# Graph attention in blocks of 1024 targets, with the two float16 halves summed in the same PSUM columns and the pair ends off GpSimd

## The chip, the cores and the metric

The kernel runs on one core of a Trainium2 chip. The metric is the device time of one execution in microseconds (us). A time given here is the median of an execution's repetitions, with the lowest and highest behind it. All runs compared here were in the fast state (mean granted TensorE clock 0.976 to 0.987 over the span, and 0.946 to 0.948 in e3).

## The reference, cut to what matters

Two graph attention (GAT) layers over 4096 nodes with 256 features and 8 heads of 32, then one transformer layer with the same adjacency. All is float32.

```python
def _gat_layer(x, adj_mat, W, a):
    Wh = jnp.einsum('nd,hdo->hno', x, W)
    src = jnp.einsum('hno,ho->hn', Wh, a[:, :O])
    dst = jnp.einsum('hno,ho->hn', Wh, a[:, O:])
    e = jax.nn.leaky_relu(src[:, :, None] + dst[:, None, :], LRELU_SLOPE)   # 0.2
    e = jnp.where(adj_mat[None, :, :] > 0, e, NEG_INF)
    alpha = jax.nn.softmax(e, axis=-1)
    out = jnp.einsum('hnm,hmo->hno', alpha, Wh)
    return jnp.transpose(out, (1, 0, 2)).reshape(N, -1)
h = jax.nn.elu(_gat_layer(x, adj_mat, W1, a1)) + x
out = jax.nn.elu(_gat_layer(h, adj_mat, W2, a2)) + h
# ... then layer norm, masked attention, projection, MLP
```

The kernel never forms the exponentials for all pairs of nodes. Where `src_n + dst_m >= 0` the weight is `exp(src_n) exp(dst_m)`, elsewhere `exp(0.2 src_n) exp(0.2 dst_m)`. So it needs only the 0/1 matrix "the sum is at least zero", masked by the adjacency, and multiplies it by rows that already carry `exp(dst)` or `exp(0.2 dst)`. Those rows are kept as two float16 halves, high and low, to come near float32.

## The kernel before

A block of targets is four or six tiles of 128. For each pair of heads (j = 0, 1) it runs over 32 tiles of sources (m), in groups of four. VectorE makes head 0's compares, ScalarE head 1's (as a sign), and VectorE ands them with the mask:

```python
TILES = (4, 6, 6, 6, 6, 4)
...
LO = 2048.0; V1 = O + 1; VW = 4 * V1        # 132: form 1 high, low, form 2 high, low
...
for i in range(G):                           # compare(), one group of four source tiles
    mt = g * G + i
    nc.vector.tensor_scalar(t8[:, i, 0, :n], s_b[:, 0, :n], L.negd[:, mt, 2 * p : 2 * p + 1],
                            None, op0=ALU.is_ge, saturate=False)
    nc.scalar.activation(t8[:, i, 1, :n].bitcast(I8), s_b[:, 1, :n], AF.Sign,
                         bias=L.negd[:, mt, 2 * p + 1 : 2 * p + 2], scale=-1.0)
    if i % 2 == 1:
        # ... both = two source tiles, both heads, as int32
        nc.vector.tensor_tensor(both, both, m32..., op=ALU.bitwise_and)
```

TensorE then does three matmuls for each target tile and source tile, 132 columns each, into one bank of PSUM (the memory in which matmuls accumulate) for each target tile:

```python
for n in range(TILES[nb]):
    for m in range(G):
        for j in range(2):
            nc.tensor.matmul(acc[n][:, j * VW : (j + 1) * VW], t8[:, m, j, at],
                             vst[g][:, m, 2 * p + j, :], start=(mt == 0 and j == 0), stop=False)
        nc.tensor.matmul(acc[n][:, 2 * VW : 3 * VW]..., masks[l, nb][mt // MC][:, mt % MC, at],
                         vst[g][:, m, 2 * p : 2 * p + 2, 2 * V1 :], start=False, stop=(mt == NT - 1))
```

ScalarE then copies the sums out of PSUM (the "evictions" below). The pair end adds the halves, combines, divides and applies the activation. It runs beside the next pair's work:

```python
nc.vector.scalar_tensor_tensor(halves[:, :, :V1], halves[:, :, V1:], 1.0 / LO, halves[:, :, :V1], ...)
nc.gpsimd.tensor_tensor(y, over, ev[...], op=ALU.subtract)
nc.gpsimd.tensor_tensor(y, y, L.r[...], op=ALU.mult)
nc.gpsimd.tensor_tensor(y, y, ev[...], op=ALU.add)
# ... check, reciprocal on VectorE
nc.gpsimd.tensor_tensor(z, y[:, :, :, :O], inv..., op=ALU.mult)
nc.vector.tensor_scalar(low, z, 0.0, None, op0=ALU.min)
nc.scalar.activation(th, low, AF.Tanh, scale=0.5)
nc.scalar.activation(low, low, AF.Exp)
nc.vector.scalar_tensor_tensor(th, low, 1.0, th, op0=ALU.add, op1=ALU.mult)
nc.vector.scalar_tensor_tensor(th, z, 0.0, th, op0=ALU.max, op1=ALU.add)
nc.gpsimd.tensor_tensor(th, th, x, op=ALU.add)
```

## Time and profile before

The time is 3616.01 us (3614.03 to 3619.31). The stages, from the times of the pairs' last evictions and of the first and last scores in the trace:

| stage | ends at, us |
|---|---|
| GAT layer 1 (first block's start and preparation included) | 986.9 |
| GAT layer 2, last matmul | 1862.6 |
| layer norms and projections, until the first scores | 2012.1 |
| last scores | 3315.9 |
| end | 3617.8 (the profiled execution) |

The change touches the first two rows directly. The groups of instructions that matter there are these, from the page's costliest groups. Engines are PE (TensorE's matmuls), PEld (its weight loads, one before each matmul), DVE (VectorE), ACT (ScalarE) and POOL (GpSimd); SPq is SyncE's queue of DMA transfers. The columns are line, engine, operation, output and input by name, shapes, count; then busy time and the mean nanoseconds of one; then the idle time before them and what ended most of it.

```profile
L1225 PE MATMUL bank<-vst,t 128*128 128x132 f16 x16384 | 1498.8, 221 | 108.0 <-DVE t L1031 78.9
L1021 ACT ACTIVATE t<-s_b,g_negd 128x768 int8<-128x768 f32 (+1 forms) x1536 | 1198.5, 854 | 73.3 <-PE bank L1225 61.7
L1013 DVE TENSOR_SCALAR t<-s_b,g_negd 128x768 fp8e4<-128x768 f32 (+1 forms) x1536 | 914.4, 647 | 7.2 <-PE bank L1225 6.2
L1031 DVE TENSOR_TENSOR t<-t,mask 128x768 int32<-128x768 int32 (+1 forms) x768 | 652.2, 869 | 1.9 <-DVE e_inv L1091 0.3
L1077 POOL TENSOR_TENSOR e_y<-ev 128x396 f32<-128x396 f32 (+1 forms) x48 | 95.0, 1980 | 1061.2 <-DVE ev L1067 1043.7
```

TensorE's matmuls waited 78.9 us for VectorE's ands, while VectorE's ands and compares waited 9 us in all: VectorE holds the layers up. The last line is one of GpSimd's five operations of a pair end.

### The profile page before, as it was taken

To read this page: it belongs to the slowest core of one execution; us is meant where nothing else is said; L and a number is where in the kernel's file an instruction comes from. 1 tells how busy PE (TensorE), PEld (TensorE's weight loads), DVE (VectorE), ACT (ScalarE), POOL (GpSimd) and SP (SyncE) were. 2 spreads that over 40 slices of the span, in tenths; PEclk is the share of its full clock that TensorE was granted. 3 is DMA by queue.
4 is the path that set the end of the run, shared out by engine and by line. 5 is a ranking of instruction groups with operands and counts; after the bars stand their busy time and mean duration, and the time that the engine had idled before them with its cause. 6 is when DMAs were issued, how large, how long until landed. Compare 5 with 4: busy or idle time off the path is not lost. (4 is left out here: it accounts for less than half of the span.)

```text
span 3617.8 us, 84393 instructions
## 1 busy us (share of the span) xinstructions
PE 3338.1 (92%) x35522; PEld 2088.3 (58%) x35522; DVE 3119.3 (86%) x4361; ACT 2694.2 (74%) x3603; POOL 1572.3 (43%) x778
## 2 busy tenths in 40 slices
PE   6899999999888999999978799999999999997999
PEld 4789998998768999999865111111111121111666
DVE  6999999999999999999972799999999999997211
ACT  5898888888768787878764677777777777775422
POOL 0112221122101112121210699999999999997110
PEclk9999999999999999999989899999999999999999
DMA  5463334433212121211126301101010101002110
GB/s 160 139 190 115 121 117 153 123 96 88 63 40 69 32 72 37 67 54 38 35 65 157 82 25 24 39 12 44 15 36 19 30 25 24 25 7 71 41 47 25
DMA packets 224375, 237.16 MB, mean 66 GB/s; under 512 B 103728, under 2 KB 183088, under 8 KB 223984
## 3 DMA queue, kind: packets, MB, share of 16 engines
q1 hardware_dynamic: 223984, 231.66, 22.5%
q8 instruction: 280, 4.59, 0.5%
q14 instruction: 111, 0.91, 0.1%
HBM read 189.15 MB, written 42.47 MB: 64 GB/s over the span
## 5 line engine op out<-in xcount | busy, mean ns | idle before, releaser
L1225 PE MATMUL bank<-vst,t 128*128 128x132 f16 x16384 | 1498.8, 221 | 108.0 <-DVE t L1031 78.9
L1232 PE MATMUL bank<-vst,mask 128*128 128x132 f16 x8192 | 1467.4, 221 | 0.0
L1225 PEld LDWEIGHTS <-t 128*128 128x128 fp8e4 x16384 | 1270.1, 96 | 148.7 <-DVE t L1031 106.4
L1578 POOL TENSOR_TENSOR u_both<-u_e 128x1024 f32<-128x1024 f32 x512 | 1200.0, 2367 | 251.6 <-DVE u_e L1487 251.4
L1487 DVE SCALAR_TENSOR_TENSOR u_e<-u_mask,u_ps 128x1024 f32<-128x1024 uint8 x1024 | 1202.0, 1216 | 98.1 <-ACT u_ps L1485 93.6
L1021 ACT ACTIVATE t<-s_b,g_negd 128x768 int8<-128x768 f32 (+1 forms) x1536 | 1198.5, 854 | 73.3 <-PE bank L1225 61.7
L1485 ACT ACTIVATE u_ps<-u_ps 128x1024 f32<-128x1024 f32 x1024 | 1010.9, 1008 | 293.5 <-PE u_ps L1478 274.6
L1013 DVE TENSOR_SCALAR t<-s_b,g_negd 128x768 fp8e4<-128x768 f32 (+1 forms) x1536 | 914.4, 647 | 7.2 <-PE bank L1225 6.2
L1232 PEld LDWEIGHTS <-mask 128*128 128x128 fp8e4 x8192 | 808.9, 99 | 0.6
L1031 DVE TENSOR_TENSOR t<-t,mask 128x768 int32<-128x768 int32 (+1 forms) x768 | 652.2, 869 | 1.9 <-DVE e_inv L1091 0.3
L1478 PE MATMUL u_ps<-u_q,u_k 128*128 128x512 f16 x2048 | 579.0, 384 | 36.8 <-DMA u_q<-half_d 21.0
L1478 PEld LDWEIGHTS <-u_k 128*128 128x128 f16 x2048 | 139.1, 97 | 742.4 <-issue 683.8
L1077 POOL TENSOR_TENSOR e_y<-ev 128x396 f32<-128x396 f32 (+1 forms) x48 | 95.0, 1980 | 1061.2 <-DVE ev L1067 1043.7
L1492 PE MATMUL u_av<-u_e,u_v 128*32 128x512 f32 x4096 | 546.3, 605 | 0.0
L1492 PE MATMUL u_dn<-u_both,u_ones 128*32 128x512 f32 x2048 | 274.0, 605 | 1.3 <-POOL u_both L1578 1.3
L1112 POOL TENSOR_TENSOR e_th<-e_th,e_x 128x384 f32<-128x384 f32 (+1 forms) x48 | 83.1, 1732 | 370.3 <-DVE e_th L1111 342.3
L1492 PEld LDWEIGHTS u_av<-u_e,u_v 128*32 128x32 f32 x4096 | 80.9, 108 | 218.3 <-issue 210.5
L1101 ACT ACTIVATE e_th<-e_low 128x384 f32<-128x384 f32 (+1 forms) x48 | 23.4, 488 | 177.1 <-DVE e_low L1100 176.6
L1655 ACT ACTIVATE u_hid<-misc,u_b 128x512 f32<-128x512 f32 x64 | 42.3, 683 | 142.6 <-PE misc L1648 142.5
L849 ACT ACTIVATE mask<-turn 128x1024 fp8e4<-128x1024 bf16 x128 | 129.5, 1013 | 21.4 <-PE turn L847 21.2
L1671 DVE TENSOR_TENSOR u_xres<-u_xres,misc 128x256 f32<-128x256 f32 x32 | 13.5, 422 | 122.7 <-PE misc L1664 122.7
L1240 ACT COPY ev<-bank 128x396 f32<-128x396 f32 x256 | 106.8, 486 | 11.5 <-PE bank L1232 11.4
(97 smaller groups left out, 1917.8 us busy)
## 6 DMA issues: line engine op xcount, KB each, us to landing
g_rows<-in_adj_dram SPq DMA_DIRECT2D x128, 512.0 KB
mask<-mask SPq DMA_DIRECT2D x32, 768.0 KB
s_b<-s_d SPq DMA_DIRECT2D x64, 384.0 KB
u_mask<-mask SPq DMA_DIRECT2D x24, 512.0 KB
s_b<-s_d SPq DMA_DIRECT2D x32, 256.0 KB
mask<-mask SPq DMA_DIRECT2D x16, 512.0 KB
half_d<-u_halves SPq DMA_DIRECT2D x32, 256.0 KB
u_k<-half_d SPq DMA_DIRECT2D x32, 256.0 KB
```

Of the source, the lines that this page charges most:

```text
L849: nc.scalar.activation(chunk[:, :, t * P : (t + 1) * P], pt, AF.Identity, saturate=False)
L1013: nc.vector.tensor_scalar(t8[:, i, 0, :n], s_b[:, 0, :n], L.negd[:, mt, 2 * p : 2 * p + 1], None, op0=ALU.is_ge, saturate=False,)
L1021: nc.scalar.activation(t8[:, i, 1, :n].bitcast(I8), s_b[:, 1, :n], AF.Sign, bias=L.negd[:, mt, 2 * p + 1 : 2 * p + 2], scale=-1.0,)
L1031: nc.vector.tensor_tensor(both, both, m32.unsqueeze(2).to_broadcast([P, 2, 2, n // 4]), op=ALU.bitwise_and,)
L1225: nc.tensor.matmul(acc[n][:, j * VW : (j + 1) * VW], t8[:, m, j, at], vst[g][:, m, 2 * p + j, :], start=(mt == 0 and j == 0), stop=False,)
L1232: nc.tensor.matmul(acc[n][:, 2 * VW : 3 * VW].rearrange("p (j v) -> p j v", j=2), masks[l, nb][mt // MC][:, mt % MC, at], vst[g][:, m, 2 * ...
L1240: nc.scalar.copy(ev[:, n].rearrange("p k v -> p (k v)"), acc[n][:, : 3 * VW])
L1478: nc.tensor.matmul(ps[:, j, :], k_st[:, h, mt * P : (mt + 1) * P], q_st[:, h, :], start=True, stop=True,)
L1485: nc.scalar.activation(ps, ps, AF.Exp, scale=SCALE)
L1487: nc.vector.scalar_tensor_tensor(e, mask, 0.0, ps, op0=ALU.not_equal, op1=ALU.mult)
L1492: nc.tensor.matmul(to[j * O : (j + 1) * O, :], lefts[j], es[j // 2][:, j % 2, :], start=start, stop=stop,)
L1578: nc.gpsimd.tensor_tensor(both, es_of[i - 1][u], es_of[i][u], op=ALU.add)
```

## The change

The intent is to make VectorE's work fewer and wider: blocks of 1024 targets, one and for each group of four source tiles, every eighth source tile's compare given to ScalarE, no more sum of the halves, a shorter activation, and no GpSimd beside VectorE. The changed code lays two target tiles into each bank of 512 columns: at 3 x 132 columns a tile they would not fit, at 3 x 66 they do. So both halves go to the same 66 columns, and PSUM adds them. For that the low half may no longer be scaled by 2048; all rows are scaled by 32 instead, and the limits on the inputs, beyond which a general path has to run afterwards, get tighter (DST_MAX from 8 to 5.1, VALUE_MAX from 20 to 12; SRC_MAX goes and R_MAX comes). The diff, cut to its core:

```diff
-TILES = (4, 6, 6, 6, 6, 4)
+TILES = ((4, 4, 8, 8, 8), (8, 8, 8, 8))          # layer 1, layer 2
-    VW = 4 * V1
+    VW = 2 * V1
-LO = 2048.0
+UP = 32.0
@@ compare()
-            nc.vector.tensor_scalar(...)           # always VectorE for head 0
+                if j == 1 or mt % MC == MC - 1:
+                    nc.scalar.activation(to.bitcast(I8), s, AF.Sign, bias=negd, scale=-1.0)
+                else:
+                    nc.vector.tensor_scalar(to, s, negd, None, op0=ALU.is_ge, saturate=False)
-            if i % 2 == 1:                         # one and for two source tiles
+        nc.vector.tensor_tensor(both, both, mask..., op=ALU.bitwise_and)   # one for four
@@ matmuls
-                    nc.tensor.matmul(acc[n][:, j * VW : (j + 1) * VW], t8[:, m, j, at], vst[g][:, m, 2 * p + j, :], ...)
+                    for k in range(2):             # high half, low half, same columns
+                        nc.tensor.matmul(sums[:, j * VW : (j + 1) * VW], t8[:, j, w, m, at],
+                                         vst[g][:, m, 2 * p + j, k * VW : (k + 1) * VW], ...)
@@ pair end
-            nc.vector.scalar_tensor_tensor(halves...)
-            nc.gpsimd.tensor_tensor(...)           # five of them
+            nc.vector.tensor_tensor(...)
-            # min, tanh, exp, (exp + 1) * tanh, max + add
+            nc.scalar.activation(ex, z, AF.Exp)
+            nc.vector.tensor_scalar(ex, ex, 1.0, -1.0, op0=ALU.min, op1=ALU.add)
+            nc.vector.scalar_tensor_tensor(ex, z, 0.0, ex, op0=ALU.max, op1=ALU.add)
@@ mask in DRAM: one buffer for each block of targets -> one for each 512 targets, 2 KB runs
```

## The prediction

> **What bounds the kernel now.** I first split the run by the page's slices, because the change touches only the graph attention layers (two layers, one after the other), not the transformer behind them.
>
> ```profile
> ## 2 busy tenths in 40 slices
> PE   6899999999888999999978799999999999997999
> PEld 4789998998768999999865111111111121111666
> DVE  6999999999999999999972799999999999997211
> ACT  5898888888768787878764677777777777775422
> ```
>
> The row of weight loads (PEld) falls off after slice 21: that is the end of graph attention. The evictions and the pair ends on VectorE place it exactly: the first layer's last pair ends at 986.9 us, the second layer's at 1863.4 us. The other 1750 us (transformer) only get their masks in another layout, so the case is 1868 us. Next I asked for busy time by stretch; this is one pair of heads on a block of six target tiles in the steady second layer:
>
> ```profile
> core 0: us, PE busy (x) PEld busy (x) DVE busy (x) ACT busy (x) POOL busy (x), PEclk, DMA share, GB/s
> 1502.00:1539.00 37.00, 34.65 (x580) 33.70 (x578) 36.97 (x56) 30.10 (x41) 7.61 (x5) 1.00 0.13 34
> ```
>
> VectorE is busy 36.97 of 37.00 us; it is the bound. TensorE (34.65) is close behind. The starts of consecutive pair ends are 37.0 us apart for six tiles (6.17 us a tile) and 26.8 us for four (6.70). In order of time on VectorE:
>
> ```profile
> 1504.37 3.69 DVE L1013 TENSOR_SCALAR t<-s_b,g_negd 128x768 fp8e4<-128x768 f32 x3
> ...
> 1524.66 2.20 DVE L1013 TENSOR_SCALAR t<-s_b,g_negd 128x768 fp8e4<-128x768 f32 x4
> 1526.78 1.81 DVE L1031 TENSOR_TENSOR t<-t,mask 128x768 int32<-128x768 int32 x2
> 1528.51 2.20 DVE L1013 TENSOR_SCALAR t<-s_b,g_negd 128x768 fp8e4<-128x768 f32 x4
> ```
>
> Undisturbed, four compares take 2.12 us start to start (0.530 each), an and 0.867. But three compares took 3.6 us at 1504.37, and there GpSimd runs its pair end:
>
> ```profile
> 1502.86 2.43 POOL L1077 TENSOR_TENSOR e_y<-ev 128x396 f32<-128x396 f32 x1 [18.87 <-DVE ev L1067]
> 1505.36 1.05 POOL L1080 TENSOR_TENSOR e_y<-e_y,g_r 128x396 f32<-128x396 f32 x1
> 1506.49 1.15 POOL L1083 TENSOR_TENSOR e_y<-e_y,ev 128x396 f32<-128x396 f32 x1
> ```
>
> A pair's budget adds up: 32 compares x 0.530 = 17.0; 16 ands x 0.867 = 13.9; pair-end work on VectorE (1.30 for the two halves' sum, six small ones) 2.9; and what GpSimd costs: 2.0 at 1504, about 0.5 beside the division, 0.8 beside the last addition. 17.0 + 13.9 + 2.9 + 3.3 = 37.1, against 37.0.
>
> TensorE's own floor, in order of time:
>
> ```profile
> 1499.98 0.22 PE L1232 MATMUL bank<-vst,mask 128*128 128x132 f16 x1
> 1499.98 0.15 PEld L1225 LDWEIGHTS <-t 128*128 128x128 fp8e4 x2
> 1500.04 0.28 PE L1225 MATMUL bank<-vst,t 128*128 128x132 f16 x2
> 1500.09 0.10 PEld L1232 LDWEIGHTS <-mask 128*128 128x128 fp8e4 x1
> 1500.15 0.22 PE L1232 MATMUL bank<-vst,mask 128*128 128x132 f16 x1
> ```
>
> Three matmuls of 132 columns in 0.175 us, 58.4 ns each, every one with its own weight load, which is hidden. 576 a pair make 33.6 us. ScalarE needs about 28 us of starts (30.1 in the records).
>
> **What the Trainium skill says.** "SBUF — State Buffer", section "Who interferes with whom": VectorE in a two-port mode, or with two SBUF inputs, and GpSimd shut each other out for whole instructions. The trace agrees (3.6 us for 1.59 us of compares). "VectorE: DVE Perf Modes", section "Mode 2×_2P": a float32 operation on one SBUF tensor does two elements a cycle of 0.96 GHz, with the outer dimension halved evenly; two-tensor operations one. Agrees: compares of 512 take 0.398 and of 768 0.530 (0.52 ns an element, 0.13 fixed), ands of 512 words 0.60 and of 768 0.867 (1.04 ns a word, 0.07 fixed). "TensorE: Matmul & The Clock Gate", section "Back-to-back issue gap": N/2.4 + 2.5 ns[...], but about 81 ns for N=128 once each matmul has its load. The trace agrees with the first (57.5 against 58.4) and not with the second. "PSUM — Partial Sum Buffer", on the zero region: a group's first matmul clears the bits of its whole bank. Hence the change sets the start flag on only the first tile of a bank; no run yet shows it.
>
> **The change part by part**, for a pair on eight tiles (1024 targets).
>
> *Matmuls.* The float16 halves, before side by side in 132 columns, become two matmuls of 66 columns on the same weights into the same 66 columns. Columns streamed stay equal (six of 66 for three of 132); instructions double: 8 tiles x 32 x 6 = 1536. By the skill's formula, an estimate, 66/2.4 + 2.5 = 30.0 ns: 46.1 us, 5.76 a tile (before 5.61). In the raw starts of the trace one 128-column load follows another after 14 ns, and small loads 7 ns apart, so the doubled loads should still hide under 27 ns of streaming. This is the step that I know least.
>
> *Compares.* 28 on VectorE (every eighth source tile's goes to ScalarE) of 1024: 0.530 + 0.132 = 0.662; 18.5 us. *Ands*: one a group, 2048 words: 2.13 + 0.07 = 2.20, eight of them 17.6 us.
>
> *Pair end, all on VectorE.* The halves' sum (1.30) goes. Three operations on 528 elements (384 take 0.46, so 0.61): 1.83; three on 512: 1.78; one two-port pass 0.40; check and reciprocal 0.28: 4.3 us. GpSimd's 3.3 us of disturbance go. VectorE: 18.5 + 17.6 + 4.3 = 40.4 us, 5.05 a tile.
>
> *ScalarE.* 36 signs at 1.05 us (0.84 for 768 start to start; records of 512 and 768 differ by 0.211) 37.8; four evictions 1.6; an exponential 0.6; the tanh is gone: 40.0 us.
>
> So TensorE becomes the bound: 46.1 us for eight tiles. For blocks of four: ScalarE 36 x 0.63 + 1.2 = 23.9, TensorE 23.0, VectorE 11.1 + 9.1 + 2.5 = 22.7, against 26.8 today. With three buffers of compared tiles a group's signs (4.2 to 5.3 us) and its and (2.2) have 11.5 us until TensorE needs them, so waits should stay small.
>
> *Second layer.* Today 1863.4 − 986.9 = 876.5 us, of which 8 x 26.8 + 16 x 37.0 = 806 is steady and 70 is preparation. After: 16 x 46.1 = 738 + 70, some more for the preparation's matmuls now lying on the bound: 815. Saves 61.
>
> *First layer.* Mask building adds 128 units at 0.60 (VectorE), 0.93 (ScalarE), 0.46 us (TensorE). Blocks 4, 4, 8, 8, 8: first block about 215 with its start of 45 and preparation of 60; second, under 32 units, ScalarE 95 + 30 = 125; two of eight tiles with 32 units, TensorE 184 + 15 = 199 each; the last 184. Sum 922, with seams 935. Saves 52.
>
> *Rest*: mask reloads in rows of 2 KB instead of 768 bytes, on queues with room (DMA at 13% in the stretch above): nothing. 3616 − 61 − 52 = 3503; I allow 10 us for waits at seams: 3513.
>
> **The rivals.** (1) *Doubled matmuls cost more than 30 ns*: loads that no longer hide, or a clock that falls with many short matmuls. For: they have half the streaming each, and the clock row dips in the first layer (0.95) where TensorE has gaps. Against: the hidden loads above, and a denser TensorE. At 33 ns a tile costs 6.3 us and everything is given back (about 3620); at 40 ns, 7.7 us: 256 tile-pairs x 1.5 = 390 us lost, 4000. (2) *VectorE stays the bound*: if the compare's output in two runs of 512 lost the two-port mode, a compare of 1024 takes 1.2 us, the pair 55 us: 6.9 a tile, about 3780. Against: both halves split evenly at the outer dimension of two. (3) *Coupling*: VectorE's and now waits for all of ScalarE's signs of a group, ScalarE carries more, and three engines stand at 40 to 46 us; with 5% lost to waits, 5.76 becomes 6.05 and the time about 3580. (4) *Better*: 28 ns a matmul gives 43 us and 3450.
>
> **Range and chances.** My sum holds in about two thirds of the cases; the seams and small waits spread it by some 40 us either way. Rivals 1 and 2 together get 15%, rival 3 about as much. So 3513, 8 in 10 between 3440 and 3640; faster by over 2% (below 3544) 0.68, within 2% 0.18, slower 0.14.
>
> **What would show it.** Right: pairs of eight tiles 46 to 47 us apart in the second layer; matmuls of 66 columns 30 ns start to start at clock 1.00; VectorE near 88% there, its compares 0.66 us with no slow ones, GpSimd idle; TensorE's waits for the and nearly gone. Wrong: matmul starts above 32 ns, a clock below 0.95, compares near 1.2 us, or TensorE waiting for the and as it does today.

## The result and the profile after

The changed kernel took 3561.51 us (3557.78 to 3563.65; four runs), the kernel before 3615.02 us (3612.5 to 3619.31) in the same rounds. A ratio here is the mean time of one kernel's fast runs over that of the other's of the same rounds, so it is not quite the ratio of the quoted medians. It is 0.985, with a 95% interval of 0.9833 to 0.9867: within 2%. The predicted range (3440 to 3640) holds the time. The point (3513) is 48 us too low, and the verdict is one to which I had given only 0.18.

| stage | before, us | after, us | difference |
|---|---|---|---|
| GAT layer 1 | 986.9 | 966.4 | −20.5 |
| GAT layer 2, to its last matmul | 875.7 | 854.2 | −21.5 |
| to the first scores | 149.5 | 132.2 | −17.3 |
| first to last scores | 1303.8 | 1305.4 | +1.6 |
| tail | 301.9 | 303.7 | +1.8 |
| sum | 3617.8 | 3561.9 | −55.9 |

The page's busy times and slices after (tenths of 40 equal slices) answer to those in the prediction:

```profile
PE 3392.7 (95%) x60099; PEld 2180.5 (61%) x60099; DVE 2857.7 (80%) x3344; ACT 2681.5 (75%) x3176; POOL 1239.4 (35%) x538
...
PE   7898999999989999999987999999999999997998
...
DVE  7999788888798888888852999999999999996111
ACT  5899898988668888888854777777777777775332
POOL 0000000000000000000000999999999999996110
```

VectorE is no longer full in the layers (8 where it had been 9), GpSimd is empty there, and TensorE has taken the bound. One pair of heads on eight tiles in the second layer, as busy time by stretch (columns as in the prediction's line: length; busy PE, PEld, DVE, ACT, POOL with counts; clock; DMA share; GB/s):

```profile
1404.00:1452.60 48.60, 48.60 (x1551) 48.60 (x1548) 41.57 (x47) 40.50 (x42) 0.00 (x0) 1.00 0.32 98
```

TensorE is busy through the whole 48.6 us, VectorE 41.6, ScalarE 40.5, with the clock at 1.00. VectorE in order of time:

```profile
1405.54 2.29 DVE L1030 TENSOR_TENSOR t<-t,mask 128x2048 int32<-128x2048 int32 x1 [1.12 <-ACT t L1025]
1407.75 2.73 DVE L1027 TENSOR_SCALAR t<-s_b,g_negd 128x1024 fp8e4<-128x1024 f32 x4
1410.59 2.29 DVE L1030 TENSOR_TENSOR t<-t,mask 128x2048 int32<-128x2048 int32 x1
...
1417.59 2.29 DVE L1030 TENSOR_TENSOR t<-t,mask 128x2048 int32<-128x2048 int32 x1 [2.72 <-ACT t L1025]
```

The and takes 2.21 us start to start, four compares 2.73 us of records (0.66 each start to start). Both are as predicted. Where VectorE now idles (brackets), it waits for ScalarE's signs, and those in turn wait for TensorE to free a buffer. TensorE in order of time, one set of six matmuls and the start of the next:

```profile
1410.03 0.29 PE L1203 MATMUL bank<-vst,t 128*128 128x66 f16 x4
1410.16 0.22 PE L1211 MATMUL bank<-vst,mask 128*128 128x66 f16 x2
1410.22 0.29 PE L1203 MATMUL bank<-vst,t 128*128 128x66 f16 x4
```

A set begins every 0.19 us. Averaged over raw starts it is 188.6 ns for six, 31.43 each, where three of 132 columns took 175 ns before. The groups after, from the page:

```profile
L1203 PE MATMUL bank<-vst,t 128*128 128x66 f16 x32768 | 1567.9, 194 | 29.2 <-issue 15.2
...
L1025 ACT ACTIVATE t<-s_b,g_negd 128x1024 int8<-128x1024 f32 (+1 forms) x1296 | 1266.2, 1048 | 212.4 <-PE bank L1203 198.5
...
L1030 DVE TENSOR_TENSOR t<-t,mask 128x2048 int32<-128x2048 int32 (+1 forms) x288 | 590.7, 2052 | 210.9 <-ACT t L1025 204.8
L1027 DVE TENSOR_SCALAR t<-s_b,g_negd 128x1024 fp8e4<-128x1024 f32 (+1 forms) x1008 | 635.3, 688 | 10.1 <-PE bank L1203 9.3
```

The wait has turned round. Before, matmuls waited for ands. Now the signs wait 198.5 us for matmuls, and the matmuls hardly wait.

So the questions are: why do short matmuls take 31.4 ns and not 30.0; what is each other part of the change worth; and where do the unforeseen 17 us before the scores come from?

### The profile page after: what moved, and what is told of

Same layout as the page of the kernel before. It is cut to its first block, busy times and chain, and to the rows that moved or that the text cites. A ratio compares the mean times of both kernels' runs of the same rounds, so it can differ in the third digit from the quotient of the medians.

```text
span 3561.9 us, 131329 instructions
## 1 busy us (share of the span) xinstructions
PE 3392.7 (95%) x60099; PEld 2180.5 (61%) x60099; DVE 2857.7 (80%) x3344; ACT 2681.5 (75%) x3176; POOL 1239.4 (35%) x538
## 4 chain that ended last, share of the span: by engine, by line
PE 77%; DVE 8%; ACT 7%; issue 3%; POOL 2%; DMA 2%; SPq 0%; DVEq 0%; ACTq 0%; POOLq 0%
PE bank L1203 26%; PE bank L1211 13%; PE u_ps L1452 11%; PE u_av L1466 11%; PE u_dn L1466 5%; DVE u_e L1461 4%; ACT t L1025 3%; PE misc L1638 3%; POOL u_both L1552 2%; PE misc L1391 2%; ACT u_ps L1459 1%; PE two L945 1%; PE misc L1622 1%; ACT stage L851 1%; PE turn L850 1%
## 5 line engine op out<-in xcount | busy, mean ns | idle before, releaser
L1203 PE MATMUL bank<-vst,t 128*128 128x66 f16 x32768 | 1567.9, 194 | 29.2 <-issue 15.2
L1203 PEld LDWEIGHTS <-t 128*128 128x128 fp8e4 x32768 | 1554.3, 98 | 38.5 <-issue 30.0
L1211 PE MATMUL bank<-vst,mask 128*128 128x66 f16 x16384 | 1554.6, 193 | 8.5 <-issue 8.3
L1025 ACT ACTIVATE t<-s_b,g_negd 128x1024 int8<-128x1024 f32 (+1 forms) x1296 | 1266.2, 1048 | 212.4 <-PE bank L1203 198.5
L1211 PEld LDWEIGHTS <-mask 128*128 128x128 fp8e4 x16384 | 1048.8, 97 | 11.1 <-issue 10.2
L1030 DVE TENSOR_TENSOR t<-t,mask 128x2048 int32<-128x2048 int32 (+1 forms) x288 | 590.7, 2052 | 210.9 <-ACT t L1025 204.8
L1027 DVE TENSOR_SCALAR t<-s_b,g_negd 128x1024 fp8e4<-128x1024 f32 (+1 forms) x1008 | 635.3, 688 | 10.1 <-PE bank L1203 9.3
L851 ACT ACTIVATE stage<-turn 128x1024 fp8e4<-128x1024 bf16 x112 | 112.2, 1018 | 0.0
L1638 PE MATMUL misc<-u_w,u_hid 128*128 128x256 f32 x512 | 111.8, 379 | 0.0
L1622 PE MATMUL misc<-ln_cols,u_w 128*128 128x512 f32 x256 | 111.2, 592 | 0.0
```

What stands on the lines that cost most here:

```text
L851: nc.scalar.activation(staged[0].rearrange("p i g n -> p (i g) n")[:, :, t * P : (t + 1) * P], pt, AF.Identity, saturate=False,)
L1025: nc.scalar.activation(to.bitcast(I8), s, AF.Sign, bias=negd, scale=-1.0)
L1027: nc.vector.tensor_scalar(to, s, negd, None, op0=ALU.is_ge, saturate=False)
L1030: nc.vector.tensor_tensor(both, both, mask.unsqueeze(1).to_broadcast(list(both.shape)), op=ALU.bitwise_and)
L1203: nc.tensor.matmul(sums[:, j * VW : (j + 1) * VW], t8[:, j, w, m, at], vst[g][:, m, 2 * p + j, k * VW : (k + 1) * VW], start=first and j = ...
L1211: nc.tensor.matmul(sums[:, 2 * VW :].rearrange("p (j v) -> p j v", j=2), masks[l, nb][g][:, w, m, at], vst[g][:, m, 2 * p : 2 * p + 2, k * ...
```

## The experiments

Twelve kernels ran, all in the fast state. The kernel before took 3613.7 to 3615.1 us beside them. Against it, at the 2% line, e3, e5, e11 and e12 count as faster, e1, e4, e6 and e9 as the same, and e2, e7, e8 and e10 are unclear; differences between two runs are read from their ratios to it.

### On the changed kernel: what holds TensorE

By position among the six, the changed kernel's matmuls follow one another after 29.2, 34.5, 32.6, 32.3, 30.0 and 30.0 ns (mean raw starts). The figure does not depend on the source tile, the target tile, the group or the head pair, and it is the same for loads with and without a semaphore wait.

**e1: rows of the halves at aligned addresses.** Each row of 66 values is padded to 72, so that the second half begins at a multiple of 16 bytes. To make room, a scratch buffer lost its double.

```diff
-    vst = [keep.tile([P, G, H, 2 * VW], F16, name=f"vst{q}") for q in range(NG)]
+    RW = 72
+    vst = [keep.tile([P, G, H, 2 * RW], F16, name=f"vst{q}") for q in range(NG)]
-            prod = some.tile([P, 2, H, V1], F32, name="g_prod")
+            prod = some.tile([P, 2, H, V1], F32, name="g_prod", bufs=1)
```

> The changed kernel with each run of 66 value columns padded to 72 (144 bytes), so that each of the four runs that a head pair's matmuls stream starts at a multiple of 16 bytes (one scratch tile goes from two buffers to one for the room). Theory A, the start of the streamed run in SBUF sets the cost of a matmul: today the starts within six are 29.2, 34.5, 32.6, 32.3, 30.0, 30.0 ns (188.6) for runs at 0, 4, 8 and 12 bytes over a multiple of 16; aligned, the first four all take about 29.2, the six 177 ns, an eight-tile pair 45.5 us instead of 48.6, and the time falls to 3470 to 3500 us. Theory B, it is the change to another stationary tile or other PSUM columns that costs: nothing moves, 188.6 ns and 3560 us.

Measured: correct, 3596.42 us (3590.63 to 3601.7), ratio to before 0.9946 (0.9933 to 0.996). The steady pairs fell by 1.0 us to 47.2, and six matmuls took 184.4 ns, with a slower one at every fourth or fifth place. The time rose all the same: the first pair of the run ended at 162.0 us instead of 130.1, and the second layer's first pair took 151.0 instead of 123.8. These are the two preparations, in which the single scratch buffer is used. That is a confound of mine. What follows: alignment is not the cause as I had stated it, since the six did not fall to their floor; what moved is which matmul stalls.

**e2: order of the six changed.** Both heads' high halves first, then both low halves, so that neighbours have other weights and other columns.

```diff
-                for j in range(2):
-                    for k in range(2):
+                for k in range(2):
+                    for j in range(2):
                         nc.tensor.matmul(
```

> The changed kernel with the four matmuls on the compared tiles in another order: high halves of both heads, then low halves of both. Theory A: each matmul keeps its cost with its operand (29, 32.6, 34.5, 32.3), the six stay at 188 to 189 ns and the time at 3560 us within 10. Theory B: no two neighbours of the four share a stationary tile or PSUM columns any more; each change costs 2 to 4 ns over 30, the six take 192 to 196 ns and the time rises to 3590 to 3620 us.

Measured: correct, 3542.8 us (3532.27 to 3547.16), ratio 0.9796 (0.9778 to 0.9814). Starts by position 29.3, 35.3, 29.2, 29.8, 30.1, 30.1 ns, 183.75 for six; second-layer pairs mostly 46.9 us. So the order of the same instructions is worth 19 us (the intervals of the two ratios, this one and the change's 0.9833 to 0.9867, do not meet), and one slow position is left. Neither theory had this figure.

**e3: high halves only.** Every low-half matmul is left out. I had expected a wrong result; the record counts it as correct. Without the low halves it is no longer the same computation, and no run here measures how much precision goes, so I take it only as a measure of what the other engines allow.

```diff
-                    for k in range(2):
+                    for k in range(1):
```

> The changed kernel without the low-half matmuls (wrong on purpose): half of TensorE's graph attention work is gone, all else stays. If TensorE is the bound of the changed kernel, an eight-tile pair falls from 48.6 us to what VectorE (my budget 40.4) and ScalarE (40.0) need, 41 to 43 us, and the time to 3370 to 3420 us. Rival, the coupling of the three engines holds the pair: pairs stay above 46 us and the time above 3500 us.

Measured: 3332.45 us (3330.29 to 3333.94), ratio 0.922 (0.9206 to 0.9234). Most of the second layer's pairs take 39.5 to 40.4 us. A stretch of it (it ends at 1591 us here):

```profile
1400.00:1560.00 160.00, 108.03 (x3053) 104.36 (x3050) 160.00 (x185) 157.55 (x165) 0.00 (x0) 0.93 0.17 49
```

With half the matmuls gone, VectorE is busy all 160 us and ScalarE 157.6. So TensorE is the bound of the changed kernel, and the prediction's budgets for VectorE (40.4) and ScalarE (40.0) were right: the layers run at them as soon as TensorE lets them.

**e5: 48 columns instead of 66.** Wrong on purpose: after the first group each matmul leaves out 18 columns, which makes the result wrong (relative error 0.47). It asks whether a load or the streaming sets the pace.

```diff
-                            sums[:, j * VW : (j + 1) * VW],
+                            sums[:, j * VW + (18 if g else 0) : (j + 1) * VW],
-                            vst[g][:, m, 2 * p + j, k * VW : (k + 1) * VW],
+                            vst[g][:, m, 2 * p + j, k * VW + (18 if g else 0) : (k + 1) * VW],
```

> The changed kernel with 18 of the 66 streamed columns left out of all matmuls but those of the first group (wrong on purpose): 48 columns, with the same number of matmuls and weight loads. The first two tests refuted both address and tile: the slow starts come every 4 to 5 matmuls in the aligned kernel, behind loads whose records grow 95, 96, 97, 98, 101 ns until the matmul stalls. Theory C, each load needs about 30.6 ns of its own, so that a matmul shorter than that waits for it: starts stay at 30.5 to 31.5 ns, pairs at 47 to 49 us and the time within 20 us of 3560. Theory D, streaming sets it[...]; pairs fall to 40 or 41 us, as without the low halves, and the time to 3350 to 3420 us. If the granted clock falls below 0.95 the test says less.

Measured: 3515.05 us (3510.02 and 3520.08), ratio 0.9728 (0.971 to 0.9745). The starts came 25 ns apart at every position (median), so a load does not need 30 ns, and that theory falls. Yet the pairs took 45 to 49 us and not 1536 x 25 = 38.4. The list of waits between 1120 and 1750 us shows why; columns are engine, group and what it waited for, then total us, times, longest:

```profile
PEld L1203 <- issue: 69.3, 78, 3.2
...
PE bank L1211 <- issue: 49.7, 36, 3.1
```

TensorE's loads stood still for nothing that the profile shows ("issue"), up to 3.2 us at a time. Between 1400 and 1600 us there are 32 such gaps of 0.28 to 3.3 us from one load to the next, 27.4 us in all. Of these, 28 (25.1 us) lie multiples of 256 TensorE instructions apart (a load counts as one, a matmul as one); the other four stand at the starts of pairs. Load and matmul together, gaps included, come every 30.76 ns (200 us / 6502). In the same stretch of waits the changed kernel shows 7.6 us of this, in 9 gaps:

```profile
PEld L1203 <- issue: 7.6, 9, 2.6
```

The Trainium skill, "Runtime: NRT & Kernel Launch", section "Instruction fetch mechanics", says that an engine's instructions come in blocks of 256 by its own DMA queue and that the cost of crossing a block is "mostly hidden". The spacing of 256 agrees. Hidden it is not at this rate, with 25.1 of 200 us. The trace also ties the gaps to the blocks. In it a DMA queue of kind "instruction" brings packets of 16384 bytes. Each of the 28 gaps ends 1.23 to 1.56 us after such a packet has landed. At the 22 crossings without a gap the packet had landed 1.23 to 2.40 us earlier; nowhere did TensorE go on sooner than 1.2 us after it. So TensorE waited for its instructions. In e5 this holds load and matmul to 30.8 ns, but the figure is no constant. Under mask building, where the DMA engines are busier (0.47 of their time), the changed kernel loses 14.1 of 430 us to such gaps, though its starts are 31.5 ns apart:

```profile
344.00:774.00 430.00, 418.33 (x12809) 417.05 (x12809) 365.32 (x430) 379.60 (x395) 0.00 (x0) 1.00 0.47 149
```

e2, at 30.6 ns, stands near that rate, but the gaps take only 9.2 of its 600 us from 1120 on (8.4 in the changed kernel): its pace there is set by the matmuls, not by the supply.

One matmul with an output that visits the same 66 columns twice would halve the instructions; it did not build (the builder refuses an output that names elements twice), so no run stands for it. A second matmul on weights already loaded was not had either: each matmul got a load of its own (60099 of each in the page). Both are left open.

**e6: pair ends back on GpSimd.** The five operations are undone, the rest of the change stays.

```diff
-            nc.vector.tensor_tensor(y, over, sums(1), op=ALU.subtract)
+            nc.gpsimd.tensor_tensor(y, over, sums(1), op=ALU.subtract)
  # ... and the other four alike
```

> The changed kernel with its five pair-end operations back on GpSimd. Theory: VectorE is no longer the bound (85% busy), so the 5 or so us a pair that its compares lose to GpSimd's port, less the 4 us of work that leave it, are taken up by its slack: 3555 to 3580 us. Rival, the pair ends are what the change gained from: the time rises to over 3600 us.

Measured: correct, 3589.2 us (3588.37 to 3590.21), ratio 0.9932 (0.9917 to 0.9947): 28 us more than with the change, between the two expectations. The last GAT matmul comes 26 us later, 20 of them in the first layer, where VectorE also builds masks; the second layer's pairs take 48.8 us, barely more. The compares' records are 877 ns instead of 747 (1400 to 1600 us). In the first layer's blocks under mask building (350 to 785 us) TensorE's loads waited 10.6 us for the mask rows that VectorE converts, a wait that the changed kernel does not show there. So this part is worth half of what the change gained, though TensorE is the bound: it matters where VectorE is near its own limit.

**e9: all of head 0's compares back on VectorE.**

```diff
-                if j == 1 or mt % MC == MC - 1:
+                if j == 1:
```

> The changed kernel with the compares of every eighth source tile given back to VectorE; the other parts of the change stay. Theory (TensorE is the bound, 48.2 to 48.9 us a pair of eight tiles, VectorE at 86% and ScalarE at 84%): VectorE gains four compares of 0.66 us, 2.65 us a pair, and stands at about 44.2 of 48.6; ScalarE loses about 4 us. Steady pairs of the second layer stay within 0.5 us of 48.6; the first layer, where mask building adds some 5 us a pair to VectorE, may lose up to 2 us a pair. Time 3555 to 3590. Rival (coupling: any engine that gets fuller holds up the others, as 5% lost to waits): pairs of 50 us or more in the second layer, time over 3600.

Measured: correct, 3574.89 us (3571.68 to 3587.28), ratio 0.989 (0.9875 to 0.9905); 13 us more than with the change. Second-layer pairs 48.2 to 50.5 us.

```profile
1400.00:1600.00 200.00, 196.83 (x6248) 196.35 (x6245) 180.18 (x206) 147.88 (x153) 0.00 (x0) 1.00 0.20 57
```

VectorE goes from 170 to 180 of 200 us and ScalarE from 165 to 148, TensorE stays the bound, and the loss is small. The time is in the range of the theory. The pairs reached past its 0.5 us, but the profiled run was the slowest of the four (3587.28 us, the others 3571.68 to 3576.18), so how much coupling there is stays open. In the profiled run the last GAT matmul came 20 us later than in the changed kernel, and 17 of these lie in the first layer.

### On the kernel before: the other parts alone

These keep the old blocks and the matmuls of 132 columns, and add the rest of the change part by part.

**e4: pair ends on VectorE**, by the same five lines as in e6, the other way.

```diff
-            nc.gpsimd.tensor_tensor(y, over, ...)
+            nc.vector.tensor_tensor(y, over, ...)
  # ... and the other four alike
```

> The kernel before with one part of the change alone: the five pair-end operations move from GpSimd to VectorE, nothing else. Theory, GpSimd's operations hold up VectorE's compares by 3.3 us a six-tile pair and the moved work costs VectorE 2.3 us: the pair falls from 37.0 to 36.0 us and the time to about 3575 us (3555 to 3600). Rival, the slow compares have another cause: VectorE gains 2.3 us of work per pair, 39.3 us, and the time rises to about 3700 us.

Measured: correct, 3592.06 us (3588.68 to 3594.16), ratio 0.9937 (0.9924 to 0.9951). Pairs of six 36.4 instead of 37.0, close to the expected 36.0; 22 us saved instead of some 40. Between 1400 and 1600 us VectorE is still the bound:

```profile
1400.00:1600.00 200.00, 190.43 (x3179) 185.70 (x3177) 198.74 (x328) 166.29 (x223) 0.00 (x0) 1.00 0.22 63
```

**e7: and every eighth source tile's compare on ScalarE.**

```diff
+            if mt % MC == MC - 1:
+                nc.scalar.activation(t8[:, i, 0, :n].bitcast(I8), s_b[:, 0, :n], AF.Sign, ...)
+            else:
                 nc.vector.tensor_scalar(t8[:, i, 0, :n], ...)
```

> The kernel before (blocks of 768, matmuls of 132 columns) with the pair ends on VectorE, as in the fourth run, and every eighth source tile's first compare on ScalarE: VectorE falls from 36.4 us a pair by 4 x 0.53 to 34.3, ScalarE rises to 33.6, TensorE needs 33.6. A pair takes 34.5 to 35.5 us, and the time 3530 to 3560 us. Rival, with three engines this close the waits between them eat it: pairs stay at 36 us and the time at 3585 us.

Measured: correct, 3545.41 us (3544.66 to 3548.44), ratio 0.9814 (0.9799 to 0.9829): 47 us less than e4. Pairs of six 35.2 in the second layer, of four 25.1.

**e8: and one and a group.**

```diff
-            if i % 2 == 1:  # and of two source tiles
+        both = t8[:, :, :, :n].bitcast(I32)   # after the loop: and of four
```

> The seventh run's kernel with one and of 1536 words per group in place of two of 768: VectorE 0.6 us a pair less, 33.7. Theory, TensorE at 132 columns (58.4 ns) is then the bound at 33.6 us: pairs 34 to 35 us (5.75 a tile against 6.04 of the changed kernel), the time 3515 to 3545 us, faster than the changed kernel. Rival: the wider and waits for four signs on ScalarE instead of two, and the pair gets longer than in the seventh run.

Measured: correct, 3539.15 us (3537.17 to 3540.79), ratio 0.9795 (0.9782 to 0.9809), 6 us less. The first layer gained (pairs of six 39.1 instead of 39.8), the second lost (35.8 instead of 35.2). Already this is below the whole change.

**e10: and the second layer's output in eight blocks of four tiles.** This asks about the 17 us before the first scores. My first reading was that pair ends on VectorE finish sooner. The runs so far had refuted it: from the last GAT matmul to the first scores, e4, e7 and e8, with ends on VectorE and the old blocks, took 149.4, 149.1 and 148.4 us, and e6, with ends on GpSimd and the new blocks, 133.4. So it goes with the blocks. In the old ones the transformer's row loads, four tiles each, cross from one buffer to another and fall into ten pieces instead of eight.

```diff
-        rows = [InputRows(nc, x)] + [Rows(nc, dram, f"rows{l}_", D) for l in range(2)]
+        rows = [InputRows(nc, x)] + [Rows(nc, dram, "rows0_", D, TILES),
+                                     Rows(nc, dram, "rows1_", D, (4,) * (N // 512))]
```

> The kernel before with its pair ends off GpSimd, the share of compares on ScalarE and one and a group (3539.15 us so far), and now the second layer's output kept in eight blocks of four tiles, so that each of the transformer's eight row loads is one piece instead of up to two. So far the stretch from the last graph attention matmul to the first scores takes 148 to 149 us in every kernel with the blocks of before (wherever its pair ends run) and 132 to 134 in every kernel with the blocks of the change. Theory R (the split row loads, in a queue behind stores that wait, bring the last layer norms late): this stretch falls to 131 to 137 us, TensorE no longer waits in its middle, time 3520 to 3530. Theory M (the transformer's masks, loaded in longer runs, make the difference): the stretch stays at 146 to 150 us and the time within 5 us of 3539.

Measured: correct, 3540.69 us (3537.06 to 3543.26), ratio 0.9798 (0.9785 to 0.9812); the stretch took 148.5 us. The theory of the split loads falls. What the traces do show is the order of the DMA queue. Before, in order of time:

```profile
1891.54 1.98 SPq L1378 DMA_DIRECT2D u_k<-half_d  x4
1893.63 7.44 SPq L1422 DMA_DIRECT2D half_d<-u_halves  x4
1901.12 0.51 SPq L743 DMA_DIRECT2D u_x<-rows  x1
```

and after:

```profile
1848.65 0.36 SPq L740 DMA_DIRECT2D u_x<-rows  x1
1849.06 1.98 SPq L1359 DMA_DIRECT2D u_k<-half_d  x4
```

The load of the fifth block's rows (u_x) stands behind four stores of halves, which wait for their data (7.44 us), in the kernel before; in the changed one it goes ahead of the key loads. It is issued 38.3 us after the last GAT matmul before and 27.8 after. In every other run with the old blocks the delay is 36.2 to 37.8 us, in every other run with the new ones 27.9 to 29.2. e10 has one piece a load and still the old order:

```profile
1812.08 1.82 SPq L1398 DMA_DIRECT2D u_k<-half_d  x4
1813.99 7.62 SPq L1442 DMA_DIRECT2D half_d<-u_halves  x4
1821.65 0.51 SPq L756 DMA_DIRECT2D u_x<-rows  x1
```

The later layer norms then come late. In the chain that ended last (the work followed back from the last instruction, each step to what released it) they stand between TensorE's matmuls near 1929, 1945 and 1964 us before, while after that chain runs from 1842 to 1931 almost through matmuls alone. That this order is the cause is read from the traces, not tested: no run changed the order alone. Why the build orders the queue differently for the two layouts stays open, and the masks' layout, the rival in the expectation, is not excluded.

**e11: and the short activation** (the change's exponential, minimum, maximum; no tanh).

```diff
-            nc.vector.tensor_scalar(low, held["z"], 0.0, None, op0=ALU.min)
-            nc.scalar.activation(th, low, AF.Tanh, scale=0.5)
-            nc.scalar.activation(low, low, AF.Exp)
+            nc.scalar.activation(ex, z, AF.Exp)
-            nc.vector.scalar_tensor_tensor(th, low, 1.0, th, op0=ALU.add, op1=ALU.mult)
-            nc.vector.scalar_tensor_tensor(th, z, 0.0, th, op0=ALU.max, op1=ALU.add)
+            nc.vector.tensor_scalar(ex, ex, 1.0, -1.0, op0=ALU.min, op1=ALU.add)
+            nc.vector.scalar_tensor_tensor(ex, z, 0.0, ex, op0=ALU.max, op1=ALU.add)
```

> The kernel of the eight row blocks, and its pair end with the change's form of the activation (one exponential, a minimum and an addition, a maximum and an addition) instead of two activations and one more VectorE pass. It takes about 0.46 us of VectorE and 0.5 us of ScalarE out of each pair of six tiles, of 35.8 us, in which VectorE is busy 95%, TensorE 96% and ScalarE 92%. Theory (the pair is held by all three and its end by ScalarE's evictions): pairs of six 35.4 to 35.7 us, time 5 to 15 us below the kernel of the eight row blocks. Rival (TensorE, 33.6 us of starts, and its wait for the evictions hold the pair): no difference over 4 us.

Measured: correct, 3508.98 us (3508.05 to 3509.9), ratio 0.971 (0.9697 to 0.9724): 32 us less than e10, twice the most that I expected. Pairs of six 35.2 instead of 35.8 in the second layer and 38.0 instead of 39.1 in the first. I had counted the busy time of the two operations that go, not the wait that goes with them. In e10, ScalarE's groups between 1400 and 1600 us have this line:

```profile
L1122 ACT ACTIVATE e_th<-e_low 128x384 f32<-128x384 f32 x6 | 3.1, 525 | 10.8 <-DVE e_low L1121 10.8
```

and in e11, in its place:

```profile
L1118 ACT ACTIVATE e_ex<-e_z 128x384 f32<-128x384 f32 x6 | 3.1, 523 | 0.0
```

ScalarE stood idle 1.8 us in each pair (10.8 / 6) before the tanh, which waited for VectorE's minimum; none of its signs ran in that time. The exponential of z itself does not wait. That this wait is what the run gained beyond its expectation is read from the two traces; no run takes out the wait alone.

**e12: and two ands a group in the second layer again.**

```diff
+            few = 2 if l else G
+            if (i + 1) % few == 0:
                 nc.vector.tensor_tensor(both, both, m32..., op=ALU.bitwise_and)
```

> The kernel with the short activation, and in the second layer two ands a group instead of one (in the first still one). With two ands the second layer's pairs of six took 35.2 us, with one 35.8; the first layer's, under mask building, 39.8 with two and 39.1 with one. Theory (one and a group makes TensorE wait for all four compares and saves VectorE only 0.07 us each, which counts where VectorE is the bound): second layer pairs 35.0 to 35.3 us, time 5 to 12 us below the kernel with one and everywhere, the fastest of all runs. Rival (the two kernels differed by chance or by where the pair end fell): no difference over 4 us.

Measured: correct, 3504.9 us (3501.41 to 3505.72), ratio 0.9696 (0.9683 to 0.9709), the fastest run with a full result, though its interval overlaps that of e11. The pairs are 35.2 us in both, so the theory falls: the 4 us lie at the start of the second layer (first pair 91.5 instead of 98.6). TensorE holds the pair now:

```profile
1400.00:1600.00 200.00, 192.88 (x3271) 191.36 (x3269) 191.15 (x315) 187.41 (x248) 0.00 (x0) 1.00 0.17 45
```

Its 576 starts of 58.4 ns make 33.6 of the 35.2 us; it waits 1.1 us for ScalarE's evictions at the start of a pair (6.8 us in that stretch, six times). VectorE (191) and ScalarE (187) are close behind.

In sum, from the kernel before: ends off GpSimd −22, compare share −47, one and −6, row blocks +1.5, short activation −32: from 3615 to 3509, and to 3505 with e12 (medians; the steps do not add to the last unit, since the rounds differ). The same parts together with the new blocks and the doubled matmuls give −54. Each part counts only as far as VectorE and ScalarE hold the layers, and the doubled matmuls end that early. No run has the blocks of 1024 without the doubled matmuls, so these two parts are judged only together.

## Why the prediction was right or wrong

**The bound moves from VectorE to TensorE: right**, shown by the stretches and by e3. Compares at 0.66 us with no slow ones, ands at 2.20, GpSimd idle, VectorE near 88% (measured 86%), no clock loss: all as predicted. The budgets of VectorE and ScalarE, 40.4 and 40.0 us, held within 1 us of the 39.5 to 40.4 that e3 showed.

**The 66-column matmul at 30.0 ns: mis-sized, and this is the step that failed.** The mechanism (TensorE's starts set the pair) was right. The 30.0 came from a formula that the page gives for an isolated matmul; it had fitted the 132 columns (57.5 against 58.4). Its term measured 31.43 ns, so 1536 make 48.3 us instead of 46.1, and the pair took 48.6. I had named it as the step that I know least, and its rival (33 ns gives everything back) lay the right way; the truth is halfway. e2 shows that 0.8 ns of it hangs on the order of the six, and e5 that 25 ns starts exist but that instructions do not come that fast. Why single positions stall by 3 to 6 ns stays open: it is not the address offset, a semaphore wait, or a load that needs 30 ns.

**The layers: 113 us predicted, 42 measured.** Of the 71 missing, the second layer lost 39 (854.2 against 815): 16 pairs x 2.5 us, the matmuls. The first lost 31 (966.4 against 935). By block it took 344, 217, 213 and 192 us, where I had 340, 199, 199 and 184 and 13 for seams. The last block is the matmuls alone (8). The two under mask building took 54.2 and 53.2 us a pair, 5 to 6 above the last block's 48.1, where I had added 3.7 of TensorE time only. The trace of these two blocks closes: 12288 matmuls at 31.5 ns make 387 us, 512 transposes of the mask at 55.8 ns make 29 (as predicted, 64 x 0.46), and 14 go to late blocks of instructions, of 430 in all. So what I had left out is the fetching of twice as many instructions, not a wait for VectorE or ScalarE (0.4 us in these blocks, for an eviction).

**"Rest: nothing": wrong by −17 us**, in my favour, in the stretch before the scores. I looked at the mask reloads and not at the order in which the transformer's loads stand in the queue. This was luck: without these 17 us the change would have gained some 36 us, a third of the 103 that I had predicted.

**Rivals.** Rival 1 came halfway. Rival 2 (compares losing their speed) did not come. Rival 3 (5% lost to waits) would have given nearly the measured time, but not for its reason: TensorE hardly waited for the other engines, and e9, which fills VectorE further, costs 13 us. Rival 4 did not come; in e5, with starts of 25 ns, load and matmul still came only every 30.8 ns. The sums of two rivals are loose: from their own costs a tile (6.3 and 6.9 us against 6.17, times 256) they come to about 3650 and 3800 us, not 3620 and 3780. The loads that I read as 14 ns apart stand 15 apart in the trace.

**What I did not ask**: what the change's parts give without its doubled matmuls. e11 and e12 beat both kernels, by 3% against the kernel before and 1.5% against the changed one (52.5 and 56.6 us of medians).

## What to carry to other kernels

Splitting one matmul into two on the same weights keeps the streamed columns equal but doubles the loads and instructions, and these must also be fetched. When TensorE stands at 94% of a stretch, as here, that spends the gain made elsewhere, so try the relief of the other engines on the old matmuls first. When an operation is taken off an engine, count the wait in front of it too: here a tanh of 0.5 us had 1.8 us of idle time before it. Where a difference appears far from the change, compare all runs by that stretch before explaining it: the blocks, not the engine of the pair ends, were what the fast ones had in common.

## What the Trainium skill lacked or had wrong

- "TensorE: Matmul & The Clock Gate", section "Back-to-back issue gap": for a stream of loads and matmuls it gives about 81 ns at 128 columns, and says that N/2.4 + 2.5 ns, the gap of an isolated matmul, counts too little there. Here 132 columns with a load each took 58.4 ns, and 66 columns 29.2 to 35.3 by position, where the formula gives 30.0: the formula is near, the 81 ns is not, and the stalls by position are not mentioned. Its issue floor of about 25 ns for up to 64 columns agrees with e5's starts.
- "Runtime: NRT & Kernel Launch", section "Instruction fetch mechanics": the crossing of a block of 256 instructions is called mostly hidden. With a load and a matmul every 25 ns it cost 25.1 of 200 us in e5; in the changed kernel 8.4 of 600 us in the second layer and 14.1 of 430 under mask building. TensorE went on no sooner than 1.2 us after a block of 16384 bytes had landed.
- No page that I used says that the same six matmuls in another order differ: 188.6 ns against 183.75, 19 us of this kernel.
